# Head norm of an attention block: the squares move from ScalarE to GpSimd, sums and root later in their step

## The chip, the cores and the metric

The kernel runs on one NeuronCore of a Trainium2 chip. The metric is the device time of one execution in microseconds (us). A core has five engines that run their own instruction queues in order and meet only through semaphores: TensorE (PE; PEld is its weight load), VectorE (DVE), ScalarE (ACT), GpSimd (POOL) and SyncE (SP), which here only issues DMAs. Each engine waits in its own queue, so an instruction that waits holds up everything behind it.

## The reference

All data is float32, x is 8 batches x 512 tokens x 512 features. Three blocks follow one another, each with a residual:

```
x = x + 0.5 * ffn(layernorm(x))       # expert-choice routing, 16 experts, one shared weight
x = x + attn(layernorm(x))
x = x + 0.5 * ffn(layernorm(x))
```

The attention is a differential one with 16 heads of width 32 and 4 key/value heads:

```
energy = einsum(q, k)                      # two maps per head, causal
scores = softmax(energy / sqrt(D))
diff   = scores[:, 0] - lam * scores[:, 1]
diff   = softmax(where(causal, NEG, diff)) # the second softmax
att    = einsum(diff, v)
att    = att * rsqrt(mean(att * att, -1) + 1e-8) * rms_w    # the head norm
out    = att.reshape(b, s, E) @ Wo
```

The head norm is what the change is about: for every token and head it needs the sum of the squares of 32 values and the inverse root of their mean plus an epsilon. The kernel never divides the second softmax by its sums z2. It leaves the values unnormalised, and the norm takes the factor out again: what stands under the root is then mean(values squared) + eps * z2 squared. So two things are squared, the values and the second sums.

## The kernel before, in words

**Stages.** The first FFN runs to about 190 us (routing, a threshold search over bits, expert products L381 beside it), then the attention, whose steady part lasts until some 1170 us, then a stretch in which the last batch's attention overlaps with the second FFN's start, and the second FFN's search, with which the kernel ends.

**The attention's loop.** The scheduler is switched off (`manual_schedule`): each engine executes in the order in which the program issues. One loop runs over blocks, and one turn of it, a *step* k, does different parts of five consecutive blocks. A batch has two *phases* (`gp` 0 and 1: two of the four key/value heads each), and a phase has 11 blocks: one for the first tile of 128 query tokens, two for the second, four each for the third and fourth. So a batch takes 22 steps. The tokens' tiles are called tile 0 to 3.

In step k the program issues, in this order:
- `turn_pe` (L882, TensorE): transposes of block k-3's weights, into two PSUM banks
- `values_pe` (L913, TensorE): weights times values of block k-4, if a unit is complete
- what is placed into the slot "short"
- `mask` (L828), `factors` (L799 on VectorE, L804 on GpSimd), `weigh` (L814, GpSimd) of block k-1
- `energies` (L777, VectorE) of block k, which read the scores' four banks and so free them
- at some steps the next block's `scores` (L761, TensorE); at others they come behind "long" or "long 2" (the table `PLACES`)
- `exps2` (L862, ScalarE) of block k-2, `exps` (L790, ScalarE) of block k
- slot "act mid", slot "mid"
- `turn_copy`: half of the transposed weights copied by VectorE (L898), half by ScalarE (L900)
- slots "long" and "long 2": the long products on TensorE (rope's projections L635, output projection L731)
- `values_out` (L926, VectorE), slot "dve", `difference` (L848, VectorE) of block k-1
- slot "act", then slot "pool"

What is in the slot "pool" gets an added dependency on the step's `difference`, so GpSimd does not begin it before VectorE has finished that.

**Finish steps.** For each batch and tile, `finish_steps` places the head norm into these slots at five offsets `o0..o4` from the phase's start:
- `square` at o0: on ScalarE the squares of the tile's values (`f_sq`, L683, 128x512) and two small ones of the second sums (`f_u`, L685, 128x16 each, scaled by `root_eps`)
- `sums` at o1, slot "short": on TensorE 4 + 8 small matmuls (L694 and L700) that add squares per head, into a bank `f_ss`
- `root` at o1, slot "act mid": on ScalarE logarithm and exponential (L707, L708), which give the inverse root `f_r`
- `turn` at o3 (L715, TensorE) and `norm` (L723, VectorE) spread it and multiply
- `pe` at o4 (L731) and `residual` (L737): the output projection, added to x

Tiles 0 and 1 of a batch finish in its second phase, at offsets (4, 5, 5, 7, 9) and (6, 7, 7, 9, 10). Tiles 2 and 3 finish in the next batch's first phase, at (0, 1, 2, 4, 5) and (3, 5, 5, 7, 8). For the last batch tiles 2 and 3 have offsets of their own. That makes 32 finishes.

**Neighbours.** GpSimd also adds the two halves of the rope (L665, 128x512), normalises the next batch (L574) and clears corners (L841). `sums`, `turn`, the projections, the values and the transposes of the norm share two PSUM banks in turn (`misc`): who takes a bank waits for the reader of the tile before the last. Rope's products are read by VectorE (L654, L656), which frees the bank; their swapped half travels by DMA (SP).

## Time and profile before

| What | Value |
|---|---|
| time, median of 3 runs | 1421.07 us (1421.06 to 1423.6) |
| span of the profiled execution | 1420.2 us; its own time was not recorded apart, the fastest runs lie 0.9 us above the span |
| busy, share of the span | PE 94%, DVE 81%, ACT 74%, POOL 48% |
| busy per 125 us in the steady part (795 to 920 us) | PE 118.7, DVE 115.0, ACT 115.4, POOL 65.5 us |
| one batch (period) of the steady part | 129.7 us |
| squares on ScalarE, all 32 finishes | L683 20.2 us, L685 16.1 us |
| root on ScalarE | L707 11.6 us, L708 10.0 us |
| sums on TensorE | L694 13.5 us, L700 13.2 us |

A row of the groups gives line, engine, operation, the tiles written and read, shapes and count, then busy time and mean duration in ns, then the idle time of the engine just before and what ended it. In a timeline a row has start, duration, engine, line, and in brackets the wait before it with its releaser. In the chain of waits a row has start, duration, engine and what ran; each piece was released by the one above it. The busy time of matmuls is modelled, so a busy TensorE may still be waiting inside a group.

### The profile page before, as it was taken

To read this page: it belongs to the slowest core of one execution; us is meant where nothing else is said; L and a number is where in the kernel's file an instruction comes from. 1 tells how busy PE (TensorE), PEld (TensorE's weight loads), DVE (VectorE), ACT (ScalarE), POOL (GpSimd) and SP (SyncE) were. 2 spreads that over 40 slices of the span, in tenths; PEclk is the share of its full clock that TensorE was granted. 3 is DMA by queue.
4 is the path that set the end of the run, shared out by engine and by line. 5 is a ranking of instruction groups with operands and counts; after the bars stand their busy time and mean duration, and the time that the engine had idled before them with its cause. 6 is when DMAs were issued, how large, how long until landed. Compare 5 with 4: busy or idle time off the path is not lost.

```text
span 1420.2 us, 30675 instructions
## 1 busy us (share of the span) xinstructions
PE 1328.5 (94%) x9774; PEld 738.4 (52%) x9774; DVE 1154.9 (81%) x4405; ACT 1047.0 (74%) x3644; POOL 685.4 (48%) x1314
## 2 busy tenths in 40 slices
PE   6999899899999999999999999999999997998998
PEld 4544444455555555555555555555455555555443
DVE  6554769899989988998999899889989989654566
ACT  3411128999899898989898998989899989844110
POOL 5433626554555455454545555554545555443230
PEclk9999988999999999999999999999999997999999
DMA  9300011000000101000000001010000001000006
GB/s 344 91 1 0 0 38 38 9 31 24 16 24 17 39 1 38 9 31 9 32 24 16 28 13 39 2 38 16 24 13 27 28 13 40 1 5 1 1 1 236
DMA packets 27554, 48.19 MB, mean 34 GB/s; under 512 B 4720, under 2 KB 6016, under 8 KB 27392
## 3 DMA queue, kind: packets, MB, share of 16 engines
q1 hardware_dynamic: 25152, 42.03, 8.3%
q10 hardware_dynamic: 2208, 4.19, 0.8%
q8 instruction: 77, 1.26, 0.4%
q14 instruction: 85, 0.70, 0.2%
q0 software_dynamic: 32, 0.01, 0.0%
HBM read 16.86 MB, written 8.39 MB: 18 GB/s over the span
## 4 chain that ended last, share of the span: by engine, by line
PE 60%; ACT 13%; DVE 10%; issue 2%; POOL 0%; ACTq 0%; DVEq 0%
PE r_ps L635 18%; PE sc L761 8%; PE f_o L731 8%; ACT e L790 7%; PE tp L882 6%; PE yps L381 6%; PE av L913 4%; DVE e L777 4%; DVE t L848 3%; ACT t L862 2%; PE vps L610 2%; PE kps L403 2%; PE f_f L715 1%; ACT eT L900 1%; PE tp L325 1%
## 5 line engine op out<-in xcount | busy, mean ns | idle before, releaser
L790 ACT ACTIVATE e<-e,nb 128x192 f32<-128x192 f32 (+7 forms) x1024 | 535.5, 532 | 6.5 <-DVE nb L777 4.3
L777 DVE CUSTOM_DVE_ANT_0 e<-sc,mpos 128x192 f32<-128x192 f32 (+7 forms) x1024 | 400.8, 453 | 23.7 <-PE sc L761 16.5
L814 POOL TENSOR_SCALAR e<-e,z 128x512 f32<-128x512 f32 (+7 forms) x512 | 295.9, 590 | 16.7
L862 ACT ACTIVATE t<-t,nm 128x512 f32<-128x512 f32 (+7 forms) x512 | 270.0, 534 | 42.2 <-DVE nm L848 42.0
L761 PE MATMUL sc<-r,r 32*128 32x64 f32 (+7 forms) x2048 | 245.3, 456 | 10.8 <-DVE nb L777 4.9
L848 DVE CUSTOM_DVE_ANT_0 t<-e,z 128x512 f32<-128x512 f32 (+7 forms) x512 | 240.6, 518 | 5.1 <-POOL e L814 4.2
L635 PE MATMUL r_ps<-hT,wq_sb 128*128 128x512 f32 x512 | 235.6, 601 | 0.1
L381 PE MATMUL yps<-we,y 128*128 128x512 f32 x456 | 216.5, 612 | 1.0 <-ACT y L388 0.7
L882 PEld LDWEIGHTS tp<-ident,t 128*128 128x128 f32 x1280 | 146.5, 144 | 135.6 <-ACT eT L900 43.3
L882 PE MATMUL tp<-ident,t 128*128 128x128 f32 x1280 | 188.6, 283 | 28.1 <-ACT eT L900 26.6
L790 ACT ACTIVATION_READ_ACCUMULATOR e<-e,nb 128x1 f32 x1024 | 202.1, 197 | 0.0
L665 POOL TENSOR_TENSOR r<-r,r_sw 128x512 f32<-128x512 f32 x80 | 103.0, 1296 | 175.8 <-DVE z L799 84.2
L761 PEld LDWEIGHTS sc<-r,r 32*128 32x128 f32 x2048 | 117.4, 188 | 90.7 <-DVE nb L777 44.6
L391 POOL TENSOR_TENSOR y<-y,eb 128x512 f32<-128x512 f32 x57 | 73.1, 1283 | 164.4 <-ACT y L388 134.3
L635 PEld LDWEIGHTS r_ps<-hT,wq_sb 128*128 128x128 f32 x512 | 93.0, 190 | 113.9 <-issue 99.6
L388 ACT COPY y<-yps 128x512 f32<-128x512 f32 x57 | 33.4, 586 | 155.6 <-PE yps L381 155.6
L828 POOL TENSOR_SCALAR_AFFINE_SELECT e<-e 128x128 f32<-128x128 f32 x256 | 79.2, 316 | 99.4 <-ACT e L790 99.4
L898 DVE COPY eT<-tp 128x512 f32<-128x512 f32 (+1 forms) x176 | 112.0, 636 | 16.6 <-PE tp L882 16.6
L381 PEld LDWEIGHTS yps<-we,y 128*128 128x128 f32 x456 | 81.3, 192 | 78.4 <-issue 73.6
L731 PE MATMUL f_o<-wo_sb,f_an 128*128 128x512 f32 x256 | 118.6, 605 | 0.0
L804 POOL TENSOR_TENSOR z<-z,over 128x4 f32<-128x4 f32 (+1 forms) x192 | 38.0, 201 | 142.6 <-DVE z L799 142.5
L862 ACT ACTIVATION_READ_ACCUMULATOR t<-t,nm 128x1 f32 x512 | 100.4, 196 | 0.0
(123 smaller groups left out, 1668.6 us busy)
## 6 DMA issues: line engine op xcount, KB each, us to landing
r_sw<-r_by SPq DMA_DIRECT2D x160, 128.0 KB, 2.0
x<-in_x_dram SPq DMA_DIRECT2D x6, 1024.0 KB, 13.2
out_dram<-x SPq DMA_DIRECT2D x6, 512.0 KB, 3.2
out_dram<-x ACTq DMA_DIRECT2D x6, 512.0 KB, 3.2
x<-in_x_dram SPq DMA_DIRECT2D x8, 256.0 KB, 8.2
we<-in_expert_w_dram SPq DMA_DIRECT2D x2, 1024.0 KB, 7.7
wq_sb<-in_wq_dram SPq DMA_DIRECT2D x1, 2048.0 KB, 13.9
wo_sb<-in_wo_dram SPq DMA_DIRECT2D x8, 128.0 KB, 2.8
```

Source lines behind the costliest of these rows:

```text
L381: nc.tensor.matmul(held["yps"], buf[b][:, i, c * P : (c + 1) * P], held["we"][:, c, :], start=(c == 0), stop=(c == EC - 1),)
L635: nc.tensor.matmul(t["ps"], w[:, c, c0 : c0 + P], st["hT"][:, c, :], start=(c == 0), stop=(c == EC - 1),)
L665: return nc.gpsimd.tensor_add(t["out"], t["out"], t["sw"])
L731: nc.tensor.matmul(t["o"], t["an"][:, c, :], wo_sb[:, c // 2, c % 2, :], start=(c == 0), stop=(c == 3),)
L761: nc.tensor.matmul(u["sc"][j][:, part.cols], q[j * D : (j + 1) * D, q0 : q0 + P], kq["k"][j * D : (j + 1) * D, : part.n], start=True, stop ...
L777: nc.vector.tensor_tensor_reduce(out=u["e"][:, j, part.cols], in0=u["sc"][j][:, part.cols], in1=mpos[:, S - part.n :], scale=1.0, scalar=3 ...
L790: nc.scalar.activation(e, e, AF.Exp, bias=u["nb"][:, c : c + 1], scale=-1.0, accum_out=u["z"][:, 0, c : c + 1],)
L814: nc.gpsimd.tensor_scalar(e, e, u["z"][:, 1, c : c + 1], u["z"][:, 0, c - nr : c - nr + 1], ALU.mult, ALU.mult,)
L848: u["diff"] = nc.vector.tensor_tensor_reduce(out=u["t"][:, par, r * w : r * w + part.n], in0=u["e"][:, 2 * par, s], in1=u["e"][:, 2 * par ...
L862: nc.scalar.activation(t, t, AF.Exp, bias=u["nm"][:, par, r : r + 1], scale=-1.0, accum_out=z2[:, col : col + 1],)
L882: nc.tensor.transpose(u["tp"][par][:, o : o + P], u["t"][:, par, (r * (i + 1) + c) * P : (r * (i + 1) + c + 1) * P], ident,)
L898: nc.vector.tensor_copy(o, s)
```

## The change

The squares become three GpSimd multiplications in the slot "pool": the values by themselves (128x512), the second sums by themselves (128x16, `f_zz`), and those by a constant `eps_of` that holds the epsilon for even and odd rows (128x32, `f_u`). The sums move from the slot "short" into a new slot "sums", just ahead of "long" and behind `turn_copy`, and so also behind the next block's scores in the steps where these are issued early. The root moves from "act mid" to "act", the end of the step on ScalarE. The last batch's tiles 2 and 3 keep the old form and the old places.

```diff
     root_eps = keep.tile([P, 2], F32, name="root_eps")
     nc.vector.tensor_scalar(root_eps, parity, RMS_EPS**0.5, None, ALU.mult)
+    eps_of = keep.tile([P, 2], F32, name="eps_of")
+    nc.vector.tensor_scalar(eps_of, parity, RMS_EPS, None, ALU.mult)
...
+            def factor_tile():
+                t["u"] = tiny.tile([P, 2, 4, 4], F32, name=f"{name}_u", tag="u")
+                return t["u"].rearrange("p f c (q h) -> p (f c q) h", h=2)
+
             def square():
                 t["sq"] = home["sq"].tile([P, 4, P], F32, name=f"{name}_sq", tag="sq", bufs=2)
-
-                t["u"] = tiny.tile([P, 2, 4, 4], F32, name=f"{name}_u", tag="u")
+                first = nc.gpsimd.tensor_tensor(t["sq"], st["aT"][i], st["aT"][i], ALU.mult)
                 z2 = st["z2"][:, i * H : (i + 1) * H]
-                uh = t["u"].rearrange("p f c (q h) -> p (f c q) h", h=2)
+                zz = tiny.tile([P, H], F32, name=f"{name}_zz", tag="zz")
+                nc.gpsimd.tensor_tensor(zz, z2, z2, ALU.mult)
+                nc.gpsimd.tensor_tensor(
+                    factor_tile(), zz.unsqueeze(2).to_broadcast([P, H, 2]),
+                    eps_of.unsqueeze(1).to_broadcast([P, H, 2]), ALU.mult,
+                )
+                return first
+
+            def square_late():
+                t["sq"] = home["sq"].tile([P, 4, P], F32, name=f"{name}_sq", tag="sq", bufs=2)
+                z2 = st["z2"][:, i * H : (i + 1) * H]
+                uh = factor_tile()
                 nc.scalar.activation(t["sq"], st["aT"][i], AF.Square)
...
             o0, o1, o2, o3, o4 = os
-            at(o0, "act", square)
-            at(o1, "short", sums)
-            at(o1, "act mid", root)
+            if b == B - 1 and i > 1:
+                at(o0, "act", square_late)
+                at(o1, "short", sums)
+                at(o1, "act mid", root)
+            else:
+                at(o0, "pool", square)
+                at(o1, "sums", sums)
+                at(o1, "act", root)
...
             if u2 is not None:
                 turn_copy(u2, 1)
+            fill(k, "sums")
             fill(k, "long")
```

## The prediction

> **What bounds the kernel now.** I read the page first, then the chain of waits in order of time through one steady period, then the timeline of that period engine by engine, and last the granted clock by stretch.

> ```profile
> PE 1328.5 (94%) x9774; PEld 738.4 (52%) x9774; DVE 1154.9 (81%) x4405; ACT 1047.0 (74%) x3644; POOL 685.4 (48%) x1314
> ...
> PE 60%; ACT 13%; DVE 10%; issue 2%; POOL 0%; ACTq 0%; DVEq 0%
> ```

> Three engines share the chain that ended last; GpSimd is idle half the time and never on it. From 423 to 1171 us the kernel repeats a period of 129.7 us (one batch, 22 steps), so a change is judged by the few places per period where the finish steps of the head norm stand. The chain through the first place, ScalarE's (step 5 to 8 of a batch's second phase, tiles 0 and 1 finishing):

> ```profile
> 828.67 0.53 ACT f_sq L683
> 829.21 0.40 ACT f_u L685 x2
> ...
> 833.32 0.27 ACT f_r L707
> ...
> 835.50 2.83 ACT e L790 x8
> 838.33 0.37 ACT eT L900
> ...
> 838.74 0.55 PE tp L882 x3
> ```

> ScalarE runs here without a gap for 15 us and TensorE's transposes wait for its copy L900: squares and root do lie on the path. The second place (step 5 of the first phase, where tile 3's sums stand) belongs to VectorE and TensorE:

> ```profile
> 885.72 0.49 DVE e L777
> ...
> 886.28 2.20 PE sc L761 x6
> 888.48 3.63 PE f_o L731 x8
> ...
> 892.76 1.08 PE av L913 x16
> ...
> 893.87 0.04 DVE aT L926
> ```

> The scores take 2.20 us instead of 0.9 because each bank is released by VectorE's energies (L777). The sums of tile 3 stand just ahead, at 885.58, and fill time in which the scores would wait anyway: they are not on the chain.

> **Part 1: squares leave ScalarE.**

> ```profile
> L683 ACT ACTIVATE f_sq<-aT 128x512 f32<-128x512 f32 x32 | 20.2, 632 | 2.6 <-DVE aT L926 2.6
> L685 ACT ACTIVATE f_u<-z,root_eps 128x16 f32<-128x16 f32 x64 | 16.1, 302 | 0.0
> L665 POOL TENSOR_TENSOR r<-r,r_sw 128x512 f32<-128x512 f32 x80 | 103.0, 1296 | 175.8 <-DVE z L799 84.2 <-DVE nm L848 70.8 <-DVE r L654 14.2
> ```

> 30 of 32 finishes change (the last batch's tiles 2 and 3 keep the old form). By the chain ScalarE loses 0.53 + 0.40 = 0.93 us for each, 28 us in all, of which only tile 1's copy (828.67) is on the path. Tile 0's stands before an idle wait (ScalarE waits 1.06 us for the sums at 822.4 to 823.5), tile 2's before a wait of 1.44 us, tile 3's before one of 1.78 us (885.14): off ScalarE they save nothing.

> **Part 2: squares on GpSimd.** The first product reads and writes 128x512 float32 as L665 does: 1.30 us. The two small ones are like L804 (128x4, 0.20 us) or L1158 (128x16, 0.21); L211 (128x16) took 0.41. I take 0.22 each: 1.75 us per finish, bounds 1.7 and 2.1. They wait for the difference L848 of their step and stand behind the rope add L665 and ahead of the next block's mask (L828), factors (L804) and weighing (L814), which all move back. For tile 1:

> ```profile
> 828.97 1.31 POOL L665 TENSOR_TENSOR r<-r,r_sw 128x512 f32<-128x512 f32 x1 [2.15 <-DVE z L799]
> ...
> 830.79 1.31 POOL L814 TENSOR_SCALAR e<-e,z 128x384 f32<-128x384 f32 x2
> ...
> 887.48 1.69 POOL L814 TENSOR_SCALAR e<-e,z 128x384 f32<-128x384 f32 x2
> ```

> ```profile
> 832.27 0.61 DVE L848 CUSTOM_DVE_ANT_0 t<-e,z 128x384 f32<-128x384 f32 x1
> ...
> 889.20 0.62 DVE L848 CUSTOM_DVE_ANT_0 t<-e,z 128x384 f32<-128x384 f32 x1 [0.40 <-POOL e L814]
> ```

> The first weighing ended at 831.44; 1.75 us later is 833.19, and VectorE wants it at 832.27. So a new wait of about 1.0 us arises on VectorE. What then follows is seen at 887.48: two weighings of this size beside a difference took 1.69 instead of 1.31 us, and from the end of the first weighing to the end of the second difference 1.61 us passed (888.13 to 889.74). By that row the pair ends at 833.19 + 1.61 = 834.80 instead of 833.38: VectorE is 1.42 us late. Behind it are queued the reciprocal and the energies of step 8 (833.60 becomes 835.02); their first bias is there 0.71 us later (energy 0.61, release 0.1), at 835.73, where ScalarE starts exponentials at 835.40 today. The copy that TensorE waits for at 838.74 comes 0.33 us later. Today's first stall of TensorE there (1.40 us at 834.34) shrinks, but what it saves is waited for at 838.74.

> If GpSimd did not matter, ScalarE alone would bring that copy 0.93 us earlier, less 0.37 us because the sums of tile 0 now end behind 0.86 us of scores, at 824.35, and its root at 825.07, where the second exponentials (L862) begin at 824.70 today: -0.56 us. With the small products at their upper bound (+0.4 us) it is about +0.75. So per batch, seven batches: bounds -3.9 and +5.3 us, **taken +2.3 us**, by the row at 887.48, of the same shapes. For tiles 0, 2 and 3 the weighing ends 2.1, 3 and 2.8 us before VectorE needs it, more than 1.75: nothing.

> [...] The energies beside the new product read PSUM and one SBUF input; L665 stands in that place today and spreads only from 1.267 to 1.319 us, so I add nothing for the product itself.

> **Part 3: sums behind the scores.** All four finishes of a batch have their sums in steps whose scores are issued ahead of the long products, so the sums (chain: 0.36 + 0.22 us on TensorE) now come after the scores. For tiles 0 and 2 the scores wait for nothing and the order is indifferent. For tile 1 TensorE waits afterwards anyway (1.40 us). For tile 3 the cover is lost: TensorE idles at 885.6 until 886.28, the scores still end at 888.48 by VectorE's releases, and 0.57 us of sums push L731, the values L913 and VectorE's L926, which waits for them (893.87). Seven batches: **+4.0 us**; bounds 0 (if ScalarE or VectorE is late there anyway) and +4.2.

> **Part 4: root behind the copy.** ScalarE no longer waits for sums (19.1 us in 16 waits) ahead of L900. TensorE needs that copy early only in the first place, already counted. The sums' bank is held some 1 us longer; its next user, the values L913 of the following step, comes 0.5 us or more after the root's read. Nothing; up to +0.2 us per batch if not. In the last batch's early products one copy may come 0.6 us earlier: **-0.6 us**. The added constant is one VectorE instruction of 0.16 us beside the first loads: nothing. No DMA moves; SP's order stays.

> **The clock.**

> ```profile
> 915.40:918.81 3.41, 2.90 (x18) 1.78 (x18) 3.41 (x28) 3.41 (x19) 1.45 (x3) 1.00 0.02 5
> 918.81:922.22 3.41, 3.41 (x5) 1.34 (x5) 1.17 (x6) 3.41 (x20) 0.90 (x4) 0.50 0.02 7
> ```

> (TensorE's granted clock is the third number from the end.) In every period a stretch of 3.41 us runs at half clock just as the rope products L635 begin (5.33 us instead of 3.63): these stretches begin 129.7 us apart, at 659.4, 789.1, 918.8 and 1048.5. The products begin 0.2 us ahead of it. If the stretches keep their grid while a period gets longer by 0.9 us (6.3 us in seven batches), the products slide into the slow stretch, less of it is left to them, and half of the slide is won back in each period, until it wins all of the 0.9 us, at a slide of 1.8. The 6.3 us then shrink to 2; without it they stay. I take **-2 us**, between 0 and -4.3. One more such stretch per period would cost 1.7 us, 12 us in all.

> [...]

> **Sum:** 2.3 + 4.0 - 0.6 - 2.0 = +3.7 us. The profiled execution's span is 1420.2 us, 0.9 below the median of 1421.07; 1420.2 + 3.7 + 0.9 = 1424.8 us. The measurement can tell about 0.2%, 2.8 us.

> **Rivals.** *ScalarE's time reaches TensorE (faster).* GpSimd's later weighing is absorbed because VectorE comes later there too, and both roots leave the chain: up to 0.93 + 0.60 us in eight batches, -12 us; with ScalarE's late start and tile 3's sums still paid, -4. It decides if the difference at 832.27 moves by under 0.7 us. For it: ScalarE's unbroken 15 us chain. Against: GpSimd's slack there is 0.8 us, its new work 1.75. Result 1409 to 1417. Chance 0.25.
> *Everything is covered (same).* Tile 3's sums slip into a wait further on and the clock gives the rest back: 1419 to 1423.8. Chance 0.18.
> *A further slow-clock stretch in most periods,* since TensorE now idles 0.7 us more soon after its stall of 1.66 us that ends at 882.8 (L715 waiting for VectorE's L656), or longer small products: +8 to +15 us, 1429 to 1436. Chance 0.12.
> *My forecast,* slower by 3 to 8 us: chance 0.45. Its own range is 1424 to 1429.
> That the change doesn't do what it says is excluded by the order of the instructions: per engine they are as described.

> To hold 8 in 10 the range must take in most of the faster case and the slow clock: 1412 to 1435. Faster by over 0.2%: 0.25; within: 0.18; slower: 0.57.

> **What would show it.** Right: ScalarE busy 28 us less, GpSimd 50 us more; a wait of the difference L848 for the weighing in each batch at tile 1's step, none at the others; the transposes at 838.74 still waiting for the copy; scores of step 5 ending as before with the sums behind them and VectorE's L926 0.6 us later. Wrong: TensorE's two stalls at 834 and 838 both short and the period under 129.7 us; or small products of 0.6 us; or half-clock stretches gone or doubled.

## Result, and the profile after

The changed kernel takes 1446.39 us (median of 5 runs, 1445.52 to 1452.41) against 1421.12 us (5 runs, 1421.06 to 1423.6) for the kernel before: ratio 1.0181, 95% interval 1.0164 to 1.0199. The profiled execution took 1445.54 us, its span 1443.6 us. I had forecast 1424.8 us in a range of 1412 to 1435: the sign was right, the size far too small.

The page of the changed kernel, busy time by engine and the chain by engine:

```profile
PE 1353.5 (94%) x9774; PEld 750.2 (52%) x9774; DVE 1156.6 (80%) x4406; ACT 1024.9 (71%) x3554; POOL 722.2 (50%) x1404
...
PE 59%; DVE 13%; ACT 8%; POOL 3%; issue 2%; POOLq 0%; ACTq 0%; DVEq 0%
```

ScalarE lost 22.1 us, GpSimd gained 36.8 us; I had named 28 and 50 us as signs of being right, and the misses stay unexplained but for the squares' length below. ScalarE's share of the chain fell from 13% to 8%, and GpSimd, never on it before, has 3%. TensorE, with exactly the same 9774 products, is busy 25 us longer. That is the first thing to ask about: no work was added to it.

What the squares cost on GpSimd, and what VectorE now waits for (groups by operation with minimum, median and maximum in ns; last, a row of the waits of VectorE with total us, times, longest):

```profile
L685 POOL TENSOR_TENSOR f_sq<-aT x30: 1034/1039/1045, 299.3 to 1242.7; 128x512 f32<-128x512 f32 x30
L688 POOL TENSOR_TENSOR f_zz<-z x30: 206/214/222, 300.3 to 1243.7; 128x16 f32<-128x16 f32 x30
L689 POOL TENSOR_TENSOR f_u<-f_zz,eps_of x30: 238/240/241, 300.6 to 1244.0; 128x32 f32<-128x32 f32 x30
```

```profile
DVE t L869 <- POOL e L835: 11.4, 25, 0.6
```

A finish costs GpSimd 1.5 us, less than the 1.75 I took. VectorE's difference waits for the weighing 25 times; the kernel before had 11 such waits, and the 14 new ones are two per batch, both at tile 1's step. The chain there (start, us, what):

```profile
844.58 1.29 POOL r L667
845.87 1.00 POOL f_sq L685
...
847.87 1.70 POOL e L835 x2
...
849.59 0.62 DVE t L869
...
850.37 0.53 DVE e L798
...
851.12 3.61 PE sc L782 x8
```

The rope add, the squares, the weighing pair at 1.70 us, the difference, an energy, and then TensorE's scores: GpSimd is on the path, as the prediction's Part 2 said. But the scores take 3.61 us here. Eight such products took 1.56 us in the kernel before (at 835.64 us). Most of the difference is VectorE's pace: in batches of the experiments at full clock they take 2.85 us behind the same delay (at 976.57 us below). The rest is seen in the stretches on the grid of 3.41 us (from 290 to 1180 us every time at half clock lasts 3.41 or 6.83 us in both kernels; busy us of each engine, then granted clock, third from the end):

```profile
849.66:853.07 3.41, 2.56 (x31) 1.32 (x20) 3.35 (x12) 2.98 (x9) 1.91 (x5) 1.00 0.00 0
853.07:856.48 3.41, 3.41 (x17) 1.77 (x20) 3.36 (x12) 3.41 (x12) 1.65 (x4) 0.50 0.00 0
856.48:859.90 3.42, 3.42 (x40) 1.58 (x32) 3.00 (x9) 2.68 (x8) 0.65 (x2) 0.50 0.02 5
```

Two stretches at half clock follow the one with the gap. No such stretch stood here in the last three periods of the kernel before. In the six batches from 291 to 1094 us (from one batch's value products L612 to the next one's) the time at half clock is given below by place: tile 1's step (step 8 of the second phase), tile 3's step (step 5 of the first phase, with its sums), and the rope products (first step of the second phase).

| us at half clock in six batches | tile 1's step | tile 3's step | rope products | sum | six batches take |
|---|---|---|---|---|---|
| kernel before | 10.2 | 0 | 23.9 | 34.1 | 779.7 |
| changed kernel | 30.7 | 13.7 | 27.3 | 71.7 | 803.0 |

All of the loss, 23.3 us, lies in these batches; head and tail together differ by 0.1 us. At tile 3's step (TensorE's timeline) the scores stand behind a wait, the sums behind the scores, and the products L747 after them run at half clock, 5.34 us instead of 3.70:

```profile
768.58 2.14 PE L782 MATMUL sc<-r,r 32*128 32x384 f32 x8 [0.62 <-DVE nb L798]
770.65 0.43 PE L710 MATMUL f_ss<-f_sq,hsum 128*32 128x128 f32 x8
770.89 0.42 PE L716 MATMUL f_ss<-both,f_u 128*4 128x64 f32 x16
771.24 5.34 PE L747 MATMUL f_o<-wo_sb,f_an 128*128 128x512 f32 x8
```

### The profile page after: what moved, and what is told of

Its sections match the earlier page's. It is cut to its first block, busy times and chain, and to the rows that moved or that the text cites. A ratio compares the mean times of both kernels' runs of the same rounds, so it can differ in the third digit from the quotient of the medians.

```text
span 1443.6 us, 30683 instructions
## 1 busy us (share of the span) xinstructions
PE 1353.5 (94%) x9774; PEld 750.2 (52%) x9774; DVE 1156.6 (80%) x4406; ACT 1024.9 (71%) x3554; POOL 722.2 (50%) x1404
## 4 chain that ended last, share of the span: by engine, by line
PE 59%; DVE 13%; ACT 8%; POOL 3%; issue 2%; POOLq 0%; ACTq 0%; DVEq 0%
PE r_ps L637 17%; PE sc L782 9%; PE f_o L747 8%; PE tp L903 6%; PE yps L383 5%; ACT e L811 5%; DVE e L798 5%; PE av L934 4%; DVE t L869 4%; PE vps L612 2%; PE kps L405 2%; PE f_f L731 2%; ACT t L883 1%; POOL e L835 1%; DVE eT L919 1%
## 5 line engine op out<-in xcount | busy, mean ns | idle before, releaser
L798 DVE CUSTOM_DVE_ANT_0 e<-sc,mpos 128x192 f32<-128x192 f32 (+7 forms) x1024 | 400.8, 453 | 22.0 <-PE sc L782 14.2
L782 PE MATMUL sc<-r,r 32*128 32x64 f32 (+7 forms) x2048 | 262.3, 467 | 21.4 <-DVE nb L798 16.6
L811 ACT ACTIVATION_READ_ACCUMULATOR e<-e,nb 128x1 f32 x1024 | 193.6, 189 | 0.0
L782 PEld LDWEIGHTS sc<-r,r 32*128 32x128 f32 x2048 | 125.1, 192 | 108.9 <-DVE nb L798 62.0
L747 PE MATMUL f_o<-wo_sb,f_an 128*128 128x512 f32 x256 | 124.8, 631 | 0.0
L921 ACT COPY eT<-tp 128x512 f32<-128x512 f32 (+1 forms) x176 | 93.9, 533 | 27.3 <-PE tp L903 27.3
L849 POOL TENSOR_SCALAR_AFFINE_SELECT e<-e 128x128 f32<-128x128 f32 x256 | 73.1, 296 | 62.0 <-ACT e L811 62.0
## 6 DMA issues: line engine op xcount, KB each, us to landing
r_sw<-r_by SPq DMA_DIRECT2D x160, 128.0 KB, 2.0
x<-in_x_dram SPq DMA_DIRECT2D x6, 1024.0 KB, 13.1
wo_sb<-in_wo_dram SPq DMA_DIRECT2D x8, 128.0 KB, 3.3
```

Of the source, the lines that this page charges most:

```text
L747: nc.tensor.matmul(t["o"], t["an"][:, c, :], wo_sb[:, c // 2, c % 2, :], start=(c == 0), stop=(c == 3),)
L782: nc.tensor.matmul(u["sc"][j][:, part.cols], q[j * D : (j + 1) * D, q0 : q0 + P], kq["k"][j * D : (j + 1) * D, : part.n], start=True, stop ...
L798: nc.vector.tensor_tensor_reduce(out=u["e"][:, j, part.cols], in0=u["sc"][j][:, part.cols], in1=mpos[:, S - part.n :], scale=1.0, scalar=3 ...
L811: nc.scalar.activation(e, e, AF.Exp, bias=u["nb"][:, c : c + 1], scale=-1.0, accum_out=u["z"][:, 0, c : c + 1],)
```

## What decides a half-clock stretch

TensorE's busy time doesn't: the stretch at 849.66 us is busy for 2.56 of 3.41 us and is followed by half clock, while one of the kernel before at 751.56 us, busy for only 52%, is not. I counted otherwise. Each product counts the columns at the end of its form in the profile (384 in `32*128 32x384`), times the part of 128*128 that its form begins with (32*128 for a score, 128*32 for a value product: a quarter each), at 0.454 us for 512 columns of a 128*128 product (L731 in the prediction's chain of the second place: 8 products in 3.63 us). The sum in a stretch over 3.41 us is its fill. In the 17 kernels profiled here there are 4435 stretches between 290 and 1180 us. 163 were followed by half clock, and every one of these had a fill under 0.40; of the other 4272, 22 had. A cut at 0.385 is wrong 12 times in 4435, where never expecting half clock would be wrong 163 times; leaving the transposes out of the count makes even the best cut wrong 116 times. The two obvious rivals hardly do better than never: the best cut on TensorE's busy time is wrong 153 times, the best on its longest wait 155 times. The stretch at 849.66 has 0.31, the one at 751.56 has 0.43, the one ahead of 771.15 has 0.31. Three exceptions stand at tile 3's step of the changed kernel itself, with a fill of 0.34 to 0.35 and full clock behind; by this count the "every window under about 0.36" of an expectation below is too strong. The rule is a fit to these traces, the experiments' own among them; the experiments below test it by moving full products (128*128 with 512 columns) into the poor stretches.

A long wait isn't needed either: the longest wait of TensorE in the changed kernel's six batches is 1.66 us, and the gap in the stretch at 849.66 is 0.85 us. What tells a poor stretch in these traces is its fill, and there scores and a gap of under 1 us together brought it down to 0.31.

## Experiments

Three theories at the start. A, the clock: the change itself costs little, emptier stretches of TensorE bring half clock. B: GpSimd's delay at tile 1 is paid directly. C: the new places of sums and root are paid directly. All comparisons are with the kernel before, run beside each; "half clock" without more is the total of the profiled execution. That is one execution of several, so its half clock and its batches need not be those of the median.

**The parts one by one.**

Squares alone:

```diff
                 at(o0, "pool", square)
-                at(o1, "sums", sums)
-                at(o1, "act", root)
+                at(o1, "short", sums)
+                at(o1, "act mid", root)
```

> Squares on GpSimd, sums and root in their old places. Theory A (clock): the change costs some 4 us by itself, and the other 19 of its 23 us are stretches of 3.41 us in which TensorE runs at half clock (90 us of them in the kernel before, 129 us in the changed one; span less half of that time: 1375.0 and 1379.3 us). The stretch at tile 1's step comes from GpSimd's delay and stays, the one at tile 3's step comes from the sums behind the scores and goes: 1430 to 1440 us, 105 to 120 us at half clock, span less half of it 1375 to 1379. Theory B (GpSimd's delay is on the path and is paid directly, some 3 us per batch): 1440 to 1447 us. Theory C (the sums' new place is paid directly): 1419 to 1424 us.

Measured: 1434.27 us, ratio 1.0069 (1.0041 to 1.0096), runs from 1423 to 1437; 105 us at half clock. As A said, but the spread says that one execution's profile is not the whole. The two runs under 1425 us have a granted clock of 0.974 and 0.975, the six others 0.963 and 0.964, so the amount of half clock differs from run to run; that the batches fall differently on the grid is my reading.

Places alone:

```diff
-                at(o0, "pool", square)
+                at(o0, "act", square_late)
                 at(o1, "sums", sums)
                 at(o1, "act", root)
```

> Squares on ScalarE as before, sums and root in their new places. Theory A (clock): tile 3's step loses activity and tile 1's does not: 1424 to 1434 us, 95 to 110 us at half clock, span less half of it 1375 to 1379 (tile 3's sums, 4 us, are in it). Theory B (GpSimd's delay): 1417 to 1423 us. Theory C (places): 1440 to 1447 us.

Measured: 1439.48 us, ratio 1.0110 (1.0090 to 1.0131), 104.5 us at half clock, span less half of it 1387.5. A's half clock was right and its time was not: C's range was nearer. The parts do not add up either: 12 and 17 us alone, 25 together.

Tile 1 in the old form:

```diff
-            if b == B - 1 and i > 1:
+            if i == 1 or b == B - 1 and i > 1:
```

> As changed, but tile 1 of each batch keeps its squares on ScalarE and its sums and root in the old places. Theory A (clock): the half-clock stretch at tile 1's step goes, tile 3's may stay: 1422 to 1436 us, 90 to 112 us at half clock. Theory B (GpSimd's delay at tile 1's weighing is paid directly): 1420 to 1427 us, whatever the clock does. Theory C (places): three of four tiles still have them: 1438 to 1447 us.

Measured: 1441.57 us, ratio 1.0139 (1.0124 to 1.0155), 114.6 us at half clock, 30.7 of it at the rope products in the six batches. Outside A's range, in C's. So A as I first put it, with 4 us of direct cost, is wrong. Half clock at tile 1's step falls from 30.7 to 6.8 us in the six batches, but A had said that it goes. It took half of the time at half clock for its price; the next runs show that to be too much.

**Filling the gap.** The values of one step computed twice, ahead of the waiting scores:

```diff
             if u3 is not None and u3["last"]:
                 values_pe(u3)
+                if k % 22 == 19:
+                    values_do(u3)
...
```

Here `values_do` holds the products of `values_pe`, which issues them once as before.

> As changed, but in step 8 of each batch's second phase TensorE computes the values L934 twice (the same 12 products again into the same bank), 0.75 us more work per batch just ahead of the scores that wait 0.85 us for VectorE; no other engine has more to do. Theory A (clock): with the gap filled the 3.41-us window there holds enough products, its half clock goes: FASTER than the changed kernel by 5 to 14 us (1432 to 1441 us) though TensorE has 6 us more work, 100 to 118 us at half clock. Theories B and C (delays paid directly, half clock a by-product): 1446 to 1452 us, no faster.

Measured: 1439.86 us, ratio 1.0123 (1.0108 to 1.0138): faster than the changed kernel by 6.5 us with more work (the intervals of the ratios lie apart), as only A expected. The time at half clock, 93.5 us, fell further than A had said (100 to 118). TensorE's timeline in a batch at full clock (start, us, instructions, [idle before, releaser]):

```profile
974.00 0.87 PE L903 MATMUL tp<-ident,t 128*128 128x128 f32 x6
974.80 1.58 PE L939 MATMUL av<-eT,v 128*32 128x128 f32 x48
976.57 2.85 PE L782 MATMUL sc<-r,r 32*128 32x448 f32 x8 [0.18 <-DVE nb L798]
```

48 value products where 24 stood, and the wait of 0.85 us is down to 0.18. In the six batches the half clock at tile 1's step is gone (30.7 to 0 us), at tile 3's too; at the rope products it stays (23.9).

The same doubling in the kernel before, as a control:

> Control for the values computed twice: the same doubling in the kernel before, where no half-clock stretch stands at that step. Theory A (clock): nothing to win there, only 0.75 us more work per batch: 1421 to 1430 us, 82 to 105 us at half clock. If the doubling made the changed kernel faster for another reason than the clock, it does so here too: 1411 to 1417 us.

Measured: 1423.39 us, ratio 1.0002 (0.9991 to 1.0012). The time is as A expected, the half clock (80.6 us) just under it. The doubling is no gain by itself, and hardly a cost.

**Moving work instead of adding it.** In the kernel before, one number in the table that places the next block's scores:

```diff
-        PLACES = (1, 0, 1, 2, 2, 0, 0, 0, 0, 0, 2, 0, 0, ...
+        PLACES = (1, 0, 1, 2, 2, 0, 0, 0, 0, 0, 2, 1, 0, ...
```

> The kernel before with one order changed: in the first step of each batch's second phase the next block's scores are issued between the two halves of the rope products' first tile instead of ahead of both. Same work. In the stretch of 3.41 us ahead of the half-clock one TensorE has only small scores there (0.24 of its full rate of multiplications, where every window under about 0.36 in all kernels so far was followed by half clock). Theory A (clock): two full products come into that stretch, the half-clock stretch goes in most periods: 1409 to 1416 us, 56 to 72 us at half clock instead of 90. Theory B (TensorE's order is indifferent as long as VectorE gets its scores, half clock is a by-product): 1419 to 1425 us.

Measured: 1413.43 us, ratio 0.9933 (0.9920 to 0.9947), 73.7 us at half clock (A had 56 to 72), and none at the rope products in the six batches (23.9 before). TensorE there:

```profile
911.58 0.66 PE L882 MATMUL tp<-ident,t 128*128 128x128 f32 x4 [0.40 <-ACT eT L900]
912.07 1.88 PE L635 MATMUL r_ps<-hT,wk_sb 128*128 128x512 f32 x4
913.88 1.55 PE L761 MATMUL sc<-r,r 32*128 32x192 f32 x16
915.36 1.98 PE L635 MATMUL r_ps<-hT,wk_sb 128*128 128x512 f32 x4
```

The 16 scores, 3.03 us at the pace of VectorE's energies when they stood first (785.92 us in the kernel before), take 1.55 us, behind four full products (L635, 1.88 us together); that VectorE gets ahead in that time is my reading. The same work in another order is 9 us faster.

This kernel also gives what was missing: whole batches without any half clock. They take 128.1 and 128.2 us, against 129.6 to 130.9 in the kernel before. With such batches the direct price can be read without guessing the clock's.

**The changed kernel, its parts, and the direct price.** Each with that order, so that batches without half clock occur.

This order is called the first order from here on. The changed kernel with it:

> The changed kernel with only the scores of the second phase's first step later; tile 3's sums stay behind the scores and ahead of L747. Theory A (clock): half clock stays at tile 1's step and at tile 3's place, and goes at the rope products: 1428 to 1440 us, 95 to 118 us at half clock. My prediction's direct price for tile 3's sums, 0.57 us per batch, is seen in batches without half clock: 128.9 to 129.1 us instead of 128.4 us with both orders changed; if the price is wrong, 128.4 us.

Measured: 1431.50 us, ratio 1.0068 (1.0040 to 1.0097). Four batches without half clock, 129.8 to 129.9 us: longer than either number expected. The profiled execution, 1427.12 us of runs from 1425.88 to 1441.58, has 66.8 us at half clock, where A expected 95 to 118; at tile 3's place one stretch is left in six batches. The changed kernel with the values twice, without this order, had two such batches, at 129.8 and 129.9 us: in the changed kernel the order itself neither gains nor costs at full clock. For the kernel before this is not shown, since without this order it has no batch without half clock.

Squares alone:

> Squares on GpSimd, sums and root in their old places, and in the first step of the second phase the scores later as in the kernel before with its scores later. Theory A (clock): 1408 to 1420 us, 60 to 90 us at half clock, span less half of it 1375 as for both kernels it is made of. Theory B (GpSimd's delay is paid directly): 1434 us or more, as squares alone were.

Measured: 1422.97 us, ratio 1.0001 (0.9989 to 1.0013); above what A expected and below what B did. Batches without half clock: 129.1 us. One reason is a new wait (waits of TensorE from 300 to 1175 us):

```profile
PE f_ss L710 <- POOL f_sq L685: 7.3, 7, 1.0
```

With the sums in their old place TensorE waits for GpSimd's squares themselves, 1.0 us in each batch. The later place takes this wait away, so the two parts overlap in their price.

Places alone:

> Squares on ScalarE, sums and root in their new places, scores of the second phase's first step later. Theory A (clock): the stretch at tile 3's place stays in some batches, that at the rope products goes: 1415 to 1428 us, 70 to 95 us at half clock; batches without half clock take 128.1 us (the kernel before with its scores later) + 0.57 for tile 3's sums = 128.7 us. If the places cost nothing by themselves: 128.1 us.

Measured: 1429.36 us, ratio 1.0045 (1.0032 to 1.0059); just above A's range; batches without half clock 129.2 us, 0.5 us more than tile 3's sums explain.

Root alone (Part 4; in all batches but the last):

```diff
-            at(o1, "act mid", root)
+            at(o1, "act" if b < B - 1 else "act mid", root)
```

> The kernel before with the scores of the second phase's first step later, and the root (not the sums) behind the copies on ScalarE in all batches but the last: part 4 of the change alone. In the kernel before with its scores later TensorE waits 1.4 us for the copy L900 at tile 1's step. If ScalarE's time reaches TensorE (my rival of a faster kernel): that wait falls under 0.8 us, batches without half clock take 127.3 to 127.7 us instead of 128.1, 1406 to 1411 us. If VectorE is what comes next: 128.1 us, 1411 to 1416 us. Theory A adds that the half-clock stretch at tile 1's step, which stands behind this wait, comes in fewer batches than the four of six there.

Measured: 1416.98 us, ratio 0.9959 (0.9946 to 0.9973); batches without half clock 128.1, 128.1 and 128.5 us. The values at tile 1's step come 0.6 us earlier and the products behind them at the same time as without the edit: VectorE is next there. Its median lies 1 us above the range of this theory and 3.5 us above that of the kernel it was made from. Part of it may be where the stretch at tile 1's step falls. Here it comes in three of the six batches, each time 27 us from the batch's start, and these take 129.2 us. In the kernel it was made from, three of four begin at 22 us, and their batches take the 128.1 us of a batch without. The profiled executions differ by 0.6 us only, so the rest stays open.

**Tile 3's place.** In step 5 of the first phase the scores go behind the sums and the first half of L747 (`PLACES[5]` from 0 to 1), with the first order kept:

> The changed kernel with two orders changed, same work: in the first step of the second phase as in the kernel before with its scores later, and in step 5 of the first phase (tile 3's sums) the scores stand behind the sums and the first half of tile 2's products L747. Theory A (clock): the half-clock stretches of 6.83 us at the rope products and of 3.41 us at tile 3's place go, those at tile 1's step stay: 1425 to 1436 us, 85 to 108 us at half clock. Theories B and C (delays paid directly): tile 1's delay stays, the sums of tile 3 are ahead of the scores as in the kernel before; B: 1440 to 1447 us, C: 1421 to 1428 us with the half clock as it falls.

Measured: 1423.77 us, ratio 0.9997 (0.9979 to 1.0016): the changed kernel, with nothing but two orders on TensorE changed, is level with the kernel before. The time is just under A's range and inside C's; the half clock, 98.4 us, is inside A's. So this run alone does not decide between them. Half clock stays at tile 1's step alone (23.9 us in the six batches). Filling that one too, with the values twice:

> The changed kernel with both orders of the scores changed and, in addition, the values of step 8 of the second phase computed twice: the last place with half clock in the steady batches (tile 1's step) is filled. Theory A (clock): 1411 to 1419 us, 60 to 82 us at half clock, no half clock at tile 1's step; so the change's whole 23 us and the clock's share of the kernel before are gone, with 5 us more work on TensorE. Theory D (VectorE's late pair at tile 1's step is paid directly, and the half clock only fills time that is waited anyway): 1421 to 1426 us as without the doubling.

Measured: 1416.19 us, ratio 0.9960 (0.9947 to 0.9972). Tile 1's step keeps 6.8 us at half clock; batches without any take 128.4 us in both, once 128.8, so the doubling costs next to nothing. The time is A's (the half clock, 58.8 us, just under its range), and D falls.

Three more runs were for what was still open. The two orders in the kernel before:

> Control for the two orders of the scores: the kernel before with both (first step of the second phase, step 5 of the first). Batches without half clock took 128.1 us with the first order alone, 129.9 us in the changed kernel with it and 128.4 us there with both. If the second order is a gain by itself (it fills the 2.1 us in which scores wait for VectorE's energies with the first half of L747): 126.9 to 127.3 us, 1402 to 1409 us; then the changed kernel's squares and places cost 1.3 us per batch with it too. If it only undoes the cost of tile 3's sums: 128.1 us, 1410 to 1415 us.

Measured: 1407.62 us, ratio 0.9900 (0.9883 to 0.9916), the fastest kernel of the study; 127.3 us per batch without half clock. The second order is a gain of 0.8 us per batch by itself, so the changed kernel pays 128.4 - 127.3 = 1.1 us per batch even with it.

Tile 3's sums and root alone taken back, only the first order changed:

```diff
-                at(o1, "sums", sums)
-                at(o1, "act", root)
+                at(o1, "short" if i == 3 else "sums", sums)
+                at(o1, "act mid" if i == 3 else "act", root)
```

> The changed kernel with the scores of the second phase's first step later, and tile 3's sums and root back in their old places (its squares stay on GpSimd). If tile 3's sums behind the scores cost 0.58 us per batch on TensorE: batches without half clock take 129.3 us instead of 129.9; without that cost 129.9. The half clock at tile 3's place goes, that at tile 1's step stays in some batches: 1420 to 1434 us, 60 to 95 us at half clock.

Measured: 1423.15 us, ratio 0.9999 (0.9985 to 1.0013); 129.2 us, no half clock at tile 3's step. As expected.

Tile 1 alone taken back, both orders changed (the edit as in the third experiment):

> The changed kernel with both orders of the scores changed, and tile 1 in the old form (squares on ScalarE, sums and root in their old places). If VectorE's energies, late behind GpSimd's weighing at tile 1's step, carry the change's price there (0.97 us per batch with squares and places, 0.37 with the places alone): batches without half clock take 127.4 to 128.0 us instead of 128.4, and tile 1's step loses its half clock: 1405 to 1415 us. If the price is that of GpSimd's load elsewhere: 128.4 us and over 1415 us.

Measured: 1410.26 us, ratio 0.9915 (0.9900 to 0.9930); 127.8 us. Tile 1 accounts for 0.6 of the 1.1 us. Its step did not lose its half clock (20.5 us in the six batches); there the expectation was wrong.

| | median us | ratio | batch without half clock, us |
|---|---|---|---|
| before, first order | 1413.43 | 0.9933 | 128.1 to 128.2 |
| before, both orders | 1407.62 | 0.9900 | 127.3 |
| changed, first order | 1431.50 | 1.0068 | 129.8 to 129.9 |
| changed, both orders | 1423.77 | 0.9997 | 128.4 |
| squares alone, first order | 1422.97 | 1.0001 | 129.1 |
| places alone, first order | 1429.36 | 1.0045 | 129.2 |

## Why the prediction was wrong, step by step

**The account.** At full clock a batch is 1.7 us longer (129.86 against 128.16 us): 10.2 us in six batches. The rest, 13.1 us, I put to the clock. This takes the 128.16 us from the kernel before with the first order, as if that order did nothing at full clock there. It can be cross-checked: six batches of the kernel before take 779.7 - 6 x 128.16 = 10.7 us over full clock with 34.1 us at half clock, those of the changed one 803.0 - 6 x 129.86 = 23.8 us with 71.7 us. That is 0.31 and 0.33 us lost per us at half clock, nearly the same in both, and less than a half; my reading is that in part of that time TensorE would have waited anyway. My prediction had 0.9 us per batch directly (6.3 us in seven) and -2 us for the clock.

**The clock: the step that failed most.** I asked what a fixed grid of slow stretches, one per period, does to a longer period, and took -2 us, between 0 and -4.3; no run shows such a gain, and the account above has +13.1 us in its place, with half clock up from 34.1 to 71.7 us. What makes a stretch slow I did not ask, though its length was on the page and the poor stretch ahead of it could be counted. Nor was one per period the whole: the kernel before already ran 10.2 us at half clock at tile 1's step, in two of its six batches. My third rival had the mechanism (a further slow stretch in most periods, 0.12) and one of the places: the idle time soon after the stall at L715 is tile 3's, where 13.7 us at half clock came in four of the six batches. It missed the larger one, tile 1's step (30.7 us instead of 10.2), and its range ended 10 us under the result. At tile 3's place the sums stood in the time in which the scores wait, and now wait and scores fall into one stretch. At tile 1's step it is the wait of 0.85 us for the late VectorE. In the six batches of their profiled executions, squares alone and places alone have 10.2 us each at tile 1's step, no more than the kernel before, and at tile 3's 0 and 10.2 us: at tile 3's place the half clock follows the sums, at tile 1's step it grew only with both parts together. One execution of each is little, and why both are needed there is not shown. What I named as a sign against me, "half-clock stretches gone or doubled", is what happened.

**Part 2, tile 1: right up to the copy, then a term mis-sized.** The pair took 1.69 us beside the difference, as the row at 887.48 said, and VectorE's energies start 1.2 us later in their batch (I had 1.42). The copy that TensorE waits for comes 0.2 us later (I had 0.33). But I stopped there, taking the copy for what TensorE waits for. From 300 to 1175 us TensorE's waits, first in the kernel before, then in the changed one, are (total us, times, longest):

```profile
PE tp L882 <- ACT eT L900: 18.9, 24, 1.4
PE sc L761 <- DVE nb L777: 2.3, 10, 0.6
```

```profile
PE sc L782 <- DVE nb L798: 13.0, 27, 1.2
PE tp L903 <- ACT eT L921: 6.8, 19, 0.4
```

The wait for ScalarE's copy has shrunk and the one of the scores for VectorE has grown. A batch of the changed kernel with the first order, without half clock, from VectorE to TensorE's next full products (chain):

```profile
969.83 0.53 DVE e L798
...
970.62 2.93 ACT e L811 x8
973.55 0.37 ACT eT L921
...
973.97 0.55 PE tp L903 x3
974.52 1.01 PE f_f L731 x32
975.53 2.36 PE sc L782 x8
977.89 2.34 PE f_o L747 x5
```

and the same scores in the kernel before with the first order (TensorE's timeline):

```profile
964.25 1.08 PE L715 MATMUL f_f<-f_r,ident 128*32 128x128 f32 x32
965.26 1.69 PE L761 MATMUL sc<-r,r 32*128 32x512 f32 x8
966.88 0.70 PE L731 MATMUL f_o<-wo_sb,f_an 128*128 128x512 f32 x1
```

The turn of the root, f_f, comes 0.2 us late; the scores behind it take 2.36 instead of about 1.6 us. Their banks are released by VectorE's energies of the next step, and VectorE, with hardly any idle time in between, is still 1 us late there. So 0.97 us per batch are lost at tiles 0 and 1 (at the first L747 of the batch: 30.46 against 29.50 us from the batch's start), not 0.33. The late engine reaches TensorE by two ways, and I had followed the one through ScalarE only. My term was +2.3 us in seven batches; 0.97 us in each is 6.8.

**Part 3, the sums: the price of tile 3 right, two others missed.** Tile 3's place in the kernel before with the first order, then in the changed kernel with it (TensorE's timeline, both at full clock):

```profile
1010.63 0.43 PE L694 MATMUL f_ss<-f_sq,hsum 128*32 128x128 f32 x8
1010.87 0.41 PE L700 MATMUL f_ss<-both,f_u 128*4 128x64 f32 x16
1011.32 2.14 PE L761 MATMUL sc<-r,r 32*128 32x384 f32 x8
1013.39 3.70 PE L731 MATMUL f_o<-wo_sb,f_an 128*128 128x512 f32 x8
```

```profile
1022.38 2.14 PE L782 MATMUL sc<-r,r 32*128 32x384 f32 x8 [0.62 <-DVE nb L798]
1024.45 0.42 PE L710 MATMUL f_ss<-f_sq,hsum 128*32 128x128 f32 x8
1024.70 0.41 PE L716 MATMUL f_ss<-both,f_u 128*4 128x64 f32 x16
1025.03 3.70 PE L747 MATMUL f_o<-wo_sb,f_an 128*128 128x512 f32 x8
```

The scores take 2.14 us either way. Ahead of them the sums cost nothing; behind them TensorE waits 0.62 us first, and then pays for them: 0.58 us per batch, where I had 0.57. I put tiles 0 and 2 at nothing. Tile 2's sums cost 0.14 us, and in the run with the places alone tiles 0 and 1 cost 0.37: the root of tile 0 ends later and its turn with it (f_f 0.38 us later). In the changed kernel this lies inside the 0.97, since VectorE is later still. The direct price is then 0.97 + 0.14 + 0.58 = 1.69 us per batch, which closes the 1.7 us of the account.

**Part 4: right at full clock.** The root's place gives and costs nothing there (128.1 us with and without, first order).

**The rivals.** ScalarE's time did reach TensorE's values: with the root alone they come 0.6 us earlier, in the changed kernel with the first order 1.0 us earlier in their batch than in the kernel before with it. It ended there, before scores that wait for VectorE (0.87 us in the changed kernel with the first order). That tile 3's sums would slip into a wait further on did not happen: their 0.58 us is still there at the batch's end. That a faster result was possible at all was true for another reason: with one edit of the order, the kernel before is 0.7% faster.

## What to carry to other kernels

When a change opens or joins gaps on TensorE, count how full its array is in each stretch of 3.41 us, not only how long it waits: small products with a quarter of a full one's form count a quarter, and below a fill of 0.385 the next stretch ran at half clock in these traces, with 12 exceptions in 4435. Spread full products over the steps with small ones, and put them into places where scores wait for another engine: one such order took the kernel before from 90 to 73.7 us at half clock and to 0.9933 of its time. When an engine comes late, follow every way by which it releases others until one of them has slack, and read direct prices from stretches at full clock on both sides.
